# Swapping which engine multiplies two tiles by C in a scan kernel, and retiming the streams beside it

## The chip, the core and the metric

The kernel runs on one core of a Trainium2 chip. The metric is the device time of one execution in microseconds; the time of a kernel is the median of its runs. In the text PE is the matrix engine, DVE the vector engine, ACT the scalar engine, POOL GpSimd, and SP the engine whose queue issues the DMAs. Each engine takes its own instructions strictly in the order in which the program wrote them, and waits on semaphores where an operand isn't ready.

## What is computed

The reference takes eight images of 96 channels and 64 x 64 pixels through two layers. The first is a layer norm, a projection, a depthwise convolution with silu, then a selective scan in four directions over 4096 positions, a gate with silu(z), an output projection, a skip, and a convolutional channel attention with gelu. The second is attention without softmax and a feed forward with float8 rounding. Nearly all of the time goes into the scan:

```
def step(hst, inp):
    u_i, dt_i, b_i, c_i = inp
    dA = jnp.exp(dt_i[..., None] * A)
    hst = dA * hst + (dt_i * u_i)[..., None] * b_i[:, :, None, :]
    y = jnp.einsum('bkdn,bkn->bkd', hst, c_i)
    return (hst, y)
```

There are 192 channels d, 16 states n, four directions k and eight images.

## The kernel before

**Units, tiles, slots.** A chunk is 512 positions. A unit is one chunk in one direction of one image: 8 images x 4 directions x 8 chunks = 256 units, 32 per image. A unit has six tiles. A tile `hb` is 128 rows (64 channels, two states) by 4 x 512 (four states m): 128x2048. `TILES` orders them g = 0, 1 (groups of states), and in each j = 0, 1, 2 (groups of channels), so tile n and tile n + 3 have the same channels. A unit is emitted in 24 slots, one for each row m of each tile.

For a tile the steps are:

- `inputs` (L998, POOL): hb = B x du, the product with B. In the texts this is I0 to I5 by tile.
- `decays` (L1123, ACT): da = exp(delta x A) into one of four PSUM banks, issued two slots ahead of its scan.
- the scan (L1195, DVE), one per slot, 512 positions with a carry from the unit before.
- the product with C. `BANKED` says for each tile how many of its four rows DVE multiplies: there the scan writes to the bank `da`, DVE multiplies the bank by C one slot later (L1201), and ACT copies the carry (L1202). The rest is done by POOL at once for all rows left, in place (`outputs`, L1004; O0 to O5 by tile), after ACT has copied the carry (L1207).
- `sums` (L1024, PE): sums over the states. `gather` (L1046, L1049, ACT) takes the sums from PSUM.

`BANKED` has two rows; the first is for the first eight units of an image (but not of image 0), the second for all others. Before, DVE has tiles 0, 2 and 4 whole and two or three rows of tile 5; POOL has tiles 1 and 3 and the rest of tile 5.

**The plan.** `plan` writes out by hand, for each of the 24 slots, what is emitted after that slot's scan: sums and gather of the unit before, `inputs` of coming tiles, `states` (DMAs of B and C, L932), `step_sizes` (L963 on PE, L971, L973 and L975 on ACT, L977 on DVE, L980 on POOL: softplus of dt, and dt x u) for a unit two ahead, and `spread` (DMAs of delta and du, L992). Since engines are in order, the plan sets each engine's queue. Before, POOL's queue in a unit is O5 of the unit before, I2, I3, O1, I4, the product for `ua`, I5, in odd units the product for `ub`, O3, then I0 and I1 of the next unit.

**The streams.** The other stages of the network are Python generators that run beside the scan. `advance` ticks a clock after each slot and lets each stream emit its next step; a step yields the number of ticks to its successor (`PA` = 2 after a matmul). `later` puts a DMA `HOLD` = 3 ticks off, and `fetch` marks its target as landed `LAND` = 11 ticks after the request; `landed` yields ticks until then. In images 1 to 7 the back stream works on the image before, on `kit_b`, one chunk after another: `gated` (L446 to L476), `first_conv`, `second_conv`, the channel gate, `attention`, `joined`, `feed_forward`. The front stream prepares the next image (`normed`, `paired`) at 1.5 ticks for one. `norm` (L253 to L259, then L246 and L247) is a helper of many stages. `quiet` holds a silu or gelu, which needs two table loads on ACT (L275), until the slot is in `CALM`.

In `gated` a chunk is centred by PE (L446, L447), squared by ACT (L449) and multiplied by z on DVE (L450), first 128 rows, then 64; then comes a variance, the projection (L462, L463), its scaling on DVE (L465), and a norm. Streams have one PSUM bank each (`f0`, `f1`); the dt matmul of `ua` shares the bank `y01` with the sums of tiles 0, 1, 3 and 4, and that of `ub` shares `y2` with those of tiles 2 and 5.

After the last unit come the last gated chunk and the other back stages of image 7, on four kits side by side.

Of the kernel before, what the change touches and what calls it, by code (L numbers as in the profile page):

```python
# [12 lines left out]
AF = mybir.ActivationFunctionType  # L13
# [6 lines left out]
B, C, HW = 8, 96, 64  # L20
# [10 lines left out]
SPREAD = 5  # L31
HB = 6

BANKED = ((4, 0, 4, 0, 4, 2), (4, 0, 4, 0, 4, 3))

HOLD = 3
LAND = 11
# [1 line left out]
PA = 2  # L39
# [4 lines left out]
def kernel(ctx: ExitStack, tc: tile.TileContext, a, out):  # L44
# [8 lines left out]
    nc = tc.nc  # L53
# [105 lines left out]
    def landed(*parts):  # L159
        while clock[0] < max(p.ready for p in parts):  # L160
            yield 1
# [56 lines left out]
    def windowed(ap):  # L218

        return ap.rearrange("p (w i j) -> p i w j", w=8, i=8)  # L220

    def raster(ap):
        return ap.rearrange("p (i w j) -> p i w j", i=8, w=8)

    def square(ap):
        return ap.rearrange("p (r w) -> p r w", r=8)
# [22 lines left out]
    def norm(k, srcs, sq, d):  # L249

        ps = bank(k.tag, "ctr")[:C, :]
        for i, src in enumerate(srcs):
            nc.tensor.matmul(ps, cen_c, src, start=i == 0, stop=i == len(srcs) - 1)  # L253
        yield PA
        nc.scalar.activation(sq, ps, AF.Square)
        nc.scalar.copy(d, ps)  # L256
        yield 1
        ps = bank(k.tag, "var")[:C, :]
        nc.tensor.matmul(ps, ones_c, sq, start=True, stop=True)  # L259
        yield PA  # L260
        inv_std(ps, ps)
        yield 1
        return ps

    alone = [False]
    place = [None]
    CALM = (0, 1, 8, 9, 16, 17)

    def quiet():

# [135 lines left out]
    def back_end(b, s):  # L406
# [8 lines left out]
        def gated(k, cs):  # L415


            def fetch_y(c):
                fetch(k.ya, s["y"][0][0:P, bass.ts(c, T)])
                fetch(k.yb, s["y"][0][P:DY, bass.ts(c, T)])  # L420

            def fetch_z(c):
                fetch(k.za, s["zd"][0:P, bass.ts(c, T)])
                fetch(k.zb, s["zd"][P:DI, bass.ts(c, T)])

            def fetch_base(c):
                fetch(k.bs, s["base"][:, bass.ts(c, T)])

            bs, r = k.bs.t[:C], k.r[:C]
            full, low, up, early = slice(0, P), slice(0, 64), slice(64, P), 0  # L430
            for n, c in enumerate(cs):
                while c not in s["done"]:
                    yield 1
                if n == 0 or early < n:
                    fetch_y(c)
                if n == 0:
                    fetch_z(c)
                    fetch_base(c)
                after = cs[n + 1] if n + 1 < len(cs) else None
                yield from landed(k.ya, k.yb, k.za, k.zb, k.bs)  # L440
                for rows, (wa, wb_), z, sq in (
                    (full, (cen_aa, cen_x), k.za.t, k.s1),
                    (up, (cen_x[:, 0:64], cen_bb), k.zb.t, k.s2[up]),
                ):
                    ps = bank(k.tag, "dy")[rows, :]
                    nc.tensor.matmul(ps, wa, k.ya.t, start=True, stop=False)  # L446
                    nc.tensor.matmul(ps, wb_, k.yb.t, start=False, stop=True)  # L447
                    yield PA
                    nc.scalar.activation(raster(sq), windowed(ps), AF.Square)  # L449
                    nc.vector.tensor_tensor(raster(z), windowed(ps), raster(z), ALU.mult)  # L450
                    yield 1
                if after in s["done"]:
                    fetch_y(after)
                    early = n + 1
                ps = bank(k.tag, "var")[:C, :]
                nc.tensor.matmul(ps, cen_x[:, 0:C], k.s1, start=True, stop=False)
                nc.tensor.matmul(ps, cen_x[up, 0:C], k.s2[up], start=False, stop=True)
                yield PA
                inv_std(r, ps, -1.0)
                yield 1  # L460
                ps = bank(k.tag, "attn")[:C, :]
                nc.tensor.matmul(ps, wy[0], k.za.t, start=True, stop=False)  # L462
                nc.tensor.matmul(ps, wy[1][up], k.zb.t, start=False, stop=True)  # L463
                yield PA
                nc.vector.tensor_tensor(r, ps, r, ALU.mult)  # L465
                if after is not None:
                    fetch_z(after)
                later(x1d[:, bass.ts(c, T)], r)
                if early == n and after in s["done"]:
                    fetch_y(after)  # L470
                    early = n + 1
                yield 1
                rs = yield from norm(k, (r, bs), k.s1[:C], k.d1[:C])
                if after is not None:
                    fetch_base(after)
                nc.vector.tensor_tensor(k.pad[0:C, :, 1 : HW + 1], square(k.d1[:C]), square(rs), ALU.mult)  # L476
                if early == n and after in s["done"]:
                    fetch_y(after)
                    early = n + 1
                later(xld[:C, 1 + 8 * c : 9 + 8 * c, :], k.pad)  # L480
                if k.solo and n == 5:
                    fetch_rows(k.im, xld, NC - 2)
                yield 1
# [42 lines left out]
        def second_conv(k, cs):  # L526
            if not k.solo:
                for p, c in zip(k.m3, cs):
                    nearer(p, c)
            for n, c in enumerate(cs):  # L530
                yield from landed(k.m3[n % 2])
                ps = bank(k.tag, "cab2")[:C, :]
                for dx in range(3):
                    nc.tensor.matmul(  # L534
                        ps, cab2_w[:, dx, :], k.m3[n % 2].t[:, :, dx : dx + HW], start=dx == 0, stop=dx == 2
                    )
                    if dx == 1:
                        yield 1
                yield PA
                if n + 2 < len(cs):  # L540
                    nearer(k.m3[n % 2], cs[n + 2])
                t = (k.s1, k.d1)[n % 2][:C]
                nc.scalar.activation(t, ps, AF.Identity, bias=cab2_b)
                yield 1
                nc.vector.tensor_reduce(totals[:, c : c + 1], t, AX.X, ALU.add)
                later(td[:, bass.ts(c, T)], t)
                if n == len(cs) - 1:
                    sources(k, cs[0])
                yield 1
# [29 lines left out]
        def attention(k, cs):  # L579

            t, x1, bs, new = k.ya.t[:C], k.za.t[:C], k.bs.t[:C], k.r[:C]
            for n, c in enumerate(cs):
# [27 lines left out]
                for i in range(4):  # L610
                    part = lnt[:, i * (C + 1) : (i + 1) * (C + 1)]
                    nc.tensor.matmul(ps, part, part, start=i == 0, stop=i == 3)  # L612
                yield PA
                nc.vector.tensor_tensor(gram, ps, gram, ALU.add)
                if n == len(cs) - 1:
                    normed_again(k, 0, cs[0])
# [23 lines left out]
        def feed_forward(k, cs):  # L640

            for n, c in enumerate(cs):
# [1 line left out]
                yield from landed(k.ln, k.t2[n % 2])  # L644
                ps = bank(k.tag, "att")[:C, :]
                nc.tensor.matmul(ps, small["qkvf"], k.ln.t, start=True, stop=True)  # L646
                yield PA
                nc.vector.scalar_tensor_tensor(t, ps, bff, t, ALU.add, ALU.add)
                if n + 1 < len(cs):
                    normed_again(k, n + 1, cs[n + 1])  # L650
# [406 lines left out]
    def plan(u, last, nxt, third, fourth):  # L1057
# [3 lines left out]
        def put(slot, f, *args):  # L1061
            at[slot].append((f, args))

        if last:
            put(0, outputs, last, 5)
            for m in range(2):
                put(m, sums, last, (3, 4), 2 + m)
            for m in range(2):
                put(3 + m, sums, last, (5,), m)
            put(3, gather, last, 0)  # L1070
            put(7, states, u, 1, 1)
            put(7, gather, last, 1)
        for n in range(6):
            to = (u, n + 2) if n < 4 else (nxt, n - 4)
            if to[0]:
                put(4 * n + 1, inputs, *to)
        if third and u.i % 2:
            put(16, step_sizes, (nxt, third), 5)
        put(8, outputs, u, 1)
        put(16, outputs, u, 3)  # L1080
        for m in range(4):
            put(13 + m, sums, u, (0, 1), m)
            if m < 2:
                put(18 + m, sums, u, (2,), m)
                put(22 + m, sums, u, (3, 4), m)
        put(18, before, u)
        if nxt:
            put(0, spread, nxt, 0, (0, 1))
# [7 lines left out]
        if third:  # L1096
            if third.i < NC:
                put(0, fetched_dt, third)
            put(5, fetched_u, third)
            for i, slot in enumerate((6, 8, 9, 10, 11, 12)):  # L1100
                put(slot, step_sizes, (third,), i)
            if u.i % 2:
                for i, slot in enumerate((9, 11, 12, 13, 15)):
                    put(slot, step_sizes, (nxt, third), i)
                put(17, spread, nxt, 0, (2,))
                put(18, spread, nxt, 1, (2,))
            elif u.i + 3 < len(units):
                put(21, fetched_pair, third, units[u.i + 3])
# [194 lines left out]
```

## Time and profile before

| what | value |
|---|---|
| median of 3 runs | 10766.89 us (10758.35 to 10770.26) |
| the profiled execution's own time | 10764.72 us |
| its span | 10763.0 us |
| granted TensorE clock, mean | 0.841 |
| ACT busy | 7397.8 us (69%) |
| DMA queue q1, share of 16 engines | 84.5% |
| scan L1195, mean of one | 1205 to 1274 ns by form |

The span is cut into 40 slices on the page; DVE and POOL show 9 (90% or more) in all but the first and the last:

```profile
DVE  3999999999999999999999999999999999999993
ACT  4666666777676776777767776677766767666674
POOL 3999999999999999999999999999999999999991
```

A group's line reads: line, engine, operation, out<-in, shapes and count, then busy time in us and mean ns of one, then the time the engine stood idle just before these instructions and what ended it. A line of waits reads: who waited, for whom, total us, times, longest. A line of windows gives the stretch, its length, busy time and count for PE, PEld (weight loads), DVE, ACT and POOL, then the granted clock, the DMA share and GB/s. Busy times of a group can overlap a little at both ends, so that three scans of 1.27 in a row take 3.6 us.

### The profile page before, as it was taken

Reading aid. Unit: us, or ns where it says so; the run is one execution under the profiler, and the core shown is the slowest. Engines: PE = TensorE matmul, PEld = TensorE weight load, DVE = VectorE, ACT = ScalarE, POOL = GpSimd, SP = SyncE. Lnnn points to the kernel's source line nnn. Section 1 sums busy time; section 2 is a strip of 40 time slices with the busy share of each in tenths; the row PEclk is TensorE's granted clock in tenths of the full one; section 3 lists DMA queues with packets and bytes.
Section 4 is the critical chain, followed back from the end, with each engine's and each line's share of the span. In section 5 each row is a group of like instructions: output and inputs, shape, how many; then the busy total and the mean of one; then the engine's idle time right before and its main releaser. Section 6 shows DMA issues by size and latency. Waiting matters only on the chain. (4 is left out here: it accounts for less than half of the span.)

```text
span 10763.0 us, 97608 instructions
## 1 busy us (share of the span) xinstructions
PE 8423.7 (78%) x23270; PEld 2274.2 (21%) x23270; DVE 10158.1 (94%) x11126; ACT 7397.8 (69%) x15154; POOL 10118.0 (94%) x2782
## 2 busy tenths in 40 slices
PE   7777668886788867888688886888768887677677
PEld 2121112221122211222122221222112221111112
DVE  3999999999999999999999999999999999999993
ACT  4666666777676776777767776677766767666674
POOL 3999999999999999999999999999999999999991
PEclk8888788987889878998789887898778987778788
DMA  6888888998889988898888988889888898888883
GB/s 148 208 205 209 200 209 214 226 226 200 215 216 227 227 193 220 216 231 219 201 218 214 237 212 202 217 220 237 198 211 218 219 235 200 202 203 210 208 214 94
DMA packets 1095381, 2253.29 MB, mean 209 GB/s; under 512 B 435993, under 2 KB 436698, under 8 KB 963731
## 3 DMA queue, kind: packets, MB, share of 16 engines
q1 hardware_dynamic: 1094803, 2247.05, 84.5%
q8 instruction: 184, 3.01, 0.1%
q14 instruction: 394, 3.23, 0.1%
HBM read 1507.14 MB, written 336.69 MB: 171 GB/s over the span
## 5 line engine op out<-in xcount | busy, mean ns | idle before, releaser
L998 POOL TENSOR_TENSOR hb<-b,du 128x2048 f32<-128x2048 f32 x1536 | 6952.6, 4546 | 6.1 <-DMA du<-ua 5.2
L1024 PE MATMUL p<-hb,halves 128*64 128x512 f32 x12288 | 3713.8, 707 | 1053.0 <-POOL hb L1004 562.6
L1123 ACT ACTIVATE da<-delta,w_a_logs 128x512 f32<-128x512 f32 x6144 | 4164.3, 689 | 541.5 <-DVE hb L1195 447.5
L1195 DVE TENSOR_TENSOR_SCAN da<-da,carry,hb 128x512 f32<-128x512 f32 x3311 | 4164.0, 1274 | 90.7 <-ACT carry L1202 37.0
L1004 POOL TENSOR_TENSOR hb<-hb,c 128x2048 f32<-128x2048 f32 (+2 forms) x768 | 2714.3, 3534 | 222.3 <-ACT carry L1207 203.0
L1195 DVE TENSOR_TENSOR_SCAN hb<-da,carry,hb 128x512 f32<-128x512 f32 x2065 | 2547.0, 1265 | 1.8
L1201 DVE TENSOR_TENSOR hb<-da,c 128x512 f32<-128x512 f32 x3784 | 2534.0, 670 | 1.8 <-DMA c<-xd 0.9
L1202 ACT COPY carry<-da 128x1 f32<-128x1 f32 x3784 | 593.8, 157 | 2054.5 <-DVE hb L1201 2045.1
L1024 PEld LDWEIGHTS p<-hb,halves 128*64 128x64 f32 x12288 | 904.8, 157 | 3697.8 <-issue 1876.0
L313 PE MATMUL conv<-f0im,taps 97*128 97x512 f32 (+1 forms) x2088 | 867.7, 655 | 37.2 <-ACT f0pre L369 32.2
L1195 DVE TENSOR_TENSOR_SCAN da<-da,hb 128x512 f32<-128x512 f32 x473 | 566.1, 1214 | 28.0 <-POOL hb L998 26.6
L963 PE MATMUL dt<-dts,dt_w 7*128 7x512 f32 (+1 forms) x1024 | 485.9, 742 | 92.3 <-ACT carry L1207 36.2
L980 POOL TENSOR_TENSOR ua<-nat,ua 128x512 f32<-128x512 f32 x256 | 329.9, 1289 | 170.9 <-DVE nat L977 161.8
L313 PEld LDWEIGHTS conv<-f0im,taps 97*128 97x128 f32 (+1 forms) x2088 | 256.4, 173 | 588.2 <-issue 508.8
L1207 ACT COPY carry<-hb 128x4 f32<-128x4 f32 (+2 forms) x768 | 149.7, 195 | 302.1 <-DVE hb L1195 293.7
L1195 DVE TENSOR_TENSOR_SCAN hb<-da,hb 128x512 f32<-128x512 f32 x295 | 346.8, 1205 | 1.7 <-ACT carry L1202 1.7
L259 PE MATMUL var<-f1e,ones_c 96*96 96x512 f32 x350 | 225.6, 731 | 121.8 <-ACT f1e L256 68.5
L253 PE MATMUL ctr<-f1e,cen_c 96*96 96x512 f32 x402 | 218.1, 649 | 86.1 <-ACT f1e L592 34.2
L977 DVE SCALAR_TENSOR_TENSOR nat<-dt,nat 128x512 f32<-128x512 f32 x384 | 258.0, 672 | 17.9 <-ACT nat L975 12.7
L975 ACT ACTIVATE nat<-nat,one 128x512 f32<-128x512 f32 x384 | 271.8, 708 | 0.1
L497 PE MATMUL cab<-f1im,cab_w 97*32 97x512 f32 x1044 | 256.0, 603 | 12.5 <-DMA f1im<-xld 7.1
L275 ACT ACT_TABLE_LOAD x193 | 247.6, 1283 | 4.1 <-PEq L1292 0.8
(430 smaller groups left out, 7586.0 us busy)
## 6 DMA issues: line engine op xcount, KB each, us to landing
b<-xd SPq DMA_DIRECT2D x1024, 512.0 KB
c<-xd SPq DMA_DIRECT2D x1024, 512.0 KB
delta<-nat SPq DMA_DIRECT2D x1536, 128.0 KB
du<-ua SPq DMA_DIRECT2D x1024, 128.0 KB
y<-yt SPq DMA_DIRECT2D x512, 256.0 KB
u<-y SPq DMA_DIRECT2D x384, 256.0 KB
ua<-u SPq DMA_DIRECT2D x256, 256.0 KB
du<-ub SPq DMA_DIRECT2D x512, 128.0 KB
```

Of the source, the lines that this page charges most:

```text
L313: nc.tensor.matmul(ps, taps[:, t, lo : lo + n], im[:, r0 + dy : r0 + dy + 8, dx : dx + HW], start=t == 0, stop=t == 8,)
L963: nc.tensor.matmul(ps, dt_w.rearrange("r j d -> r (j d)")[32 * w.k : 32 * w.k + R + 1, d], w.dts, start=True, stop=True)
L975: nc.scalar.activation(u.nat, u.nat, AF.Ln, bias=one)
L977: nc.vector.scalar_tensor_tensor(u.nat, u.ps, 0.0, u.nat, ALU.max, ALU.add)
L980: nc.gpsimd.tensor_tensor(x, u.nat, x, ALU.mult)
L998: nc.gpsimd.tensor_tensor(hb, u.bc[0, g], u.du[j].unsqueeze(1).to_broadcast([P, G, T]), ALU.mult)
L1004: nc.gpsimd.tensor_tensor(hb, hb, u.bc[1, TILES[n][0]][:, lo:, :], ALU.mult)
L1024: nc.tensor.matmul(ps, halves, u.hb[n][:, i, :], start=TILES[n][0] == 0 and m == 0, stop=False, skip_group_check=True)
L1123: nc.scalar.activation(da[q], u.delta[j], AF.Exp, scale=a_neg[:, u.k, j, g * G + m : g * G + m + 1])
L1195: nc.vector.tensor_tensor_scan(dd if banked else x, dd, x, 0.0 if u.start else col, ALU.mult, ALU.add)
L1201: nc.vector.tensor_tensor(x, d, c, ALU.mult)
L1202: kept.append(lambda: nc.scalar.copy(col, d[:, at : at + 1]))
```

## The change

The change has two halves.

In the scan, `BANKED` gives tile 0's products with C to POOL and tile 1's to DVE. POOL's queue becomes: O5 of the unit before, I2, O0, I3, I4, I5, the product for `ua`, I0 of the next unit, in odd units the product for `ub`, O3, I1 of the next unit. The sums of tiles 0 and 1 are emitted two slots earlier, those of tile 2 one slot; gather 0 one slot later and gather 1 one slot earlier; the step sizes one or two slots earlier.

In the streams, the slots for silu and gelu change, `norm`, `second_conv`, `attention` and `feed_forward` get one tick more ahead of a DVE step, and in `gated` the multiply by z is emitted a tick ahead of the square, z and base are awaited where they are first used, and the next base is fetched earlier.

```diff
--- before.py
+++ after.py
@@ -31,7 +31,7 @@
 SPREAD = 5
 HB = 6
 
-BANKED = ((4, 0, 4, 0, 4, 2), (4, 0, 4, 0, 4, 3))
+BANKED = ((0, 4, 4, 0, 4, 2), (0, 4, 4, 0, 4, 3))
 
 HOLD = 3
 LAND = 11
@@ -259,12 +259,12 @@
         nc.tensor.matmul(ps, ones_c, sq, start=True, stop=True)
         yield PA
         inv_std(ps, ps)
-        yield 1
+        yield 2
         return ps
 
     alone = [False]
     place = [None]
-    CALM = (0, 1, 8, 9, 16, 17)
+    CALM = (4, 5, 16, 17, 18, 19)
 
     def quiet():
 
@@ -437,7 +437,7 @@
                     fetch_z(c)
                     fetch_base(c)
                 after = cs[n + 1] if n + 1 < len(cs) else None
-                yield from landed(k.ya, k.yb, k.za, k.zb, k.bs)
+                yield from landed(k.ya, k.yb)
                 for rows, (wa, wb_), z, sq in (
                     (full, (cen_aa, cen_x), k.za.t, k.s1),
                     (up, (cen_x[:, 0:64], cen_bb), k.zb.t, k.s2[up]),
@@ -446,9 +446,11 @@
                     nc.tensor.matmul(ps, wa, k.ya.t, start=True, stop=False)
                     nc.tensor.matmul(ps, wb_, k.yb.t, start=False, stop=True)
                     yield PA
-                    nc.scalar.activation(raster(sq), windowed(ps), AF.Square)
+                    yield from landed(k.za, k.zb)
                     nc.vector.tensor_tensor(raster(z), windowed(ps), raster(z), ALU.mult)
                     yield 1
+                    nc.scalar.activation(raster(sq), windowed(ps), AF.Square)
+                yield 1
                 if after in s["done"]:
                     fetch_y(after)
                     early = n + 1
@@ -461,7 +463,7 @@
                 ps = bank(k.tag, "attn")[:C, :]
                 nc.tensor.matmul(ps, wy[0], k.za.t, start=True, stop=False)
                 nc.tensor.matmul(ps, wy[1][up], k.zb.t, start=False, stop=True)
-                yield PA
+                yield PA + 1
                 nc.vector.tensor_tensor(r, ps, r, ALU.mult)
                 if after is not None:
                     fetch_z(after)
@@ -470,9 +472,12 @@
                     fetch_y(after)
                     early = n + 1
                 yield 1
-                rs = yield from norm(k, (r, bs), k.s1[:C], k.d1[:C])
+                yield from landed(k.bs)
+                steps = norm(k, (r, bs), k.s1[:C], k.d1[:C])
+                yield next(steps)
                 if after is not None:
                     fetch_base(after)
+                rs = yield from steps
                 nc.vector.tensor_tensor(k.pad[0:C, :, 1 : HW + 1], square(k.d1[:C]), square(rs), ALU.mult)
                 if early == n and after in s["done"]:
                     fetch_y(after)
@@ -541,7 +546,7 @@
                     nearer(k.m3[n % 2], cs[n + 2])
                 t = (k.s1, k.d1)[n % 2][:C]
                 nc.scalar.activation(t, ps, AF.Identity, bias=cab2_b)
-                yield 1
+                yield 2
                 nc.vector.tensor_reduce(totals[:, c : c + 1], t, AX.X, ALU.add)
                 later(td[:, bass.ts(c, T)], t)
                 if n == len(cs) - 1:
@@ -610,7 +615,7 @@
                 for i in range(4):
                     part = lnt[:, i * (C + 1) : (i + 1) * (C + 1)]
                     nc.tensor.matmul(ps, part, part, start=i == 0, stop=i == 3)
-                yield PA
+                yield PA + 1
                 nc.vector.tensor_tensor(gram, ps, gram, ALU.add)
                 if n == len(cs) - 1:
                     normed_again(k, 0, cs[0])
@@ -644,7 +649,7 @@
                 yield from landed(k.ln, k.t2[n % 2])
                 ps = bank(k.tag, "att")[:C, :]
                 nc.tensor.matmul(ps, small["qkvf"], k.ln.t, start=True, stop=True)
-                yield PA
+                yield PA + 1
                 nc.vector.scalar_tensor_tensor(t, ps, bff, t, ALU.add, ALU.add)
                 if n + 1 < len(cs):
                     normed_again(k, n + 1, cs[n + 1])
@@ -1063,26 +1068,27 @@
 
         if last:
             put(0, outputs, last, 5)
-            for m in range(2):
-                put(m, sums, last, (3, 4), 2 + m)
+            for m in range(2, 4):
+                put(m - 2, sums, last, (3, 4), m)
             for m in range(2):
                 put(3 + m, sums, last, (5,), m)
-            put(3, gather, last, 0)
+            put(4, gather, last, 0)
+            put(6, gather, last, 1)
             put(7, states, u, 1, 1)
-            put(7, gather, last, 1)
-        for n in range(6):
+        put(4, outputs, u, 0)
+        for n, slot in enumerate((0, 5, 8, 11, 15, 19)):
             to = (u, n + 2) if n < 4 else (nxt, n - 4)
             if to[0]:
-                put(4 * n + 1, inputs, *to)
+                put(slot, inputs, *to)
         if third and u.i % 2:
             put(16, step_sizes, (nxt, third), 5)
-        put(8, outputs, u, 1)
         put(16, outputs, u, 3)
         for m in range(4):
-            put(13 + m, sums, u, (0, 1), m)
-            if m < 2:
-                put(18 + m, sums, u, (2,), m)
-                put(22 + m, sums, u, (3, 4), m)
+            put(11 + m, sums, u, (0, 1), m)
+        for m in range(2):
+            put(17 + m, sums, u, (2,), m)
+        for m in range(2):
+            put(22 + m, sums, u, (3, 4), m)
         put(18, before, u)
         if nxt:
             put(0, spread, nxt, 0, (0, 1))
@@ -1097,10 +1103,10 @@
             if third.i < NC:
                 put(0, fetched_dt, third)
             put(5, fetched_u, third)
-            for i, slot in enumerate((6, 8, 9, 10, 11, 12)):
+            for i, slot in enumerate((5, 7, 8, 9, 10, 12)):
                 put(slot, step_sizes, (third,), i)
             if u.i % 2:
-                for i, slot in enumerate((9, 11, 12, 13, 15)):
+                for i, slot in enumerate((8, 10, 11, 12, 13)):
                     put(slot, step_sizes, (nxt, third), i)
                 put(17, spread, nxt, 0, (2,))
                 put(18, spread, nxt, 1, (2,))
```

## The prediction

> **What bounds the kernel now.** I read the page's shares first, then the groups, then windows over one image, then the waits inside these windows.
>
> ```profile
> span 10763.0 us, 97608 instructions
> PE 8423.7 (78%) x23270; PEld 2274.2 (21%) x23270; DVE 10158.1 (94%) x11126; ACT 7397.8 (69%) x15154; POOL 10118.0 (94%) x2782
> ```
>
> DVE and POOL are level, so no one engine is the bound. The scan stage (first L1195 at 181.0 us, last one's end at 10532.6) is 10351.6 us of the span; the rest is the start and a tail of 230 us. The groups say what the two do.
>
> ```profile
> L998 POOL TENSOR_TENSOR hb<-b,du 128x2048 f32<-128x2048 f32 x1536 | 6952.6, 4546 | 6.1 <-DMA du<-ua 5.2
> L1004 POOL TENSOR_TENSOR hb<-hb,c 128x2048 f32<-128x2048 f32 (+2 forms) x768 | 2714.3, 3534 | 222.3 <-ACT carry L1207 203.0
> L1201 DVE TENSOR_TENSOR hb<-da,c 128x512 f32<-128x512 f32 x3784 | 2534.0, 670 | 1.8 <-DMA c<-xd 0.9
> ```
>
> Over 256 units that is 6 products with B and 3 with C per unit on POOL, and 24 scans with 14.8 products on DVE. POOL waited 203 us for the carry copy L1207, that is for DVE to end a tile. Now image 3 (units 96 to 127, 4042.6 to 5341.7 us) cut at its unit 0, the gated chunks, the middle, and the feed forward; columns are PE, PEld, DVE, ACT, POOL.
>
> ```profile
> 4042.60:4080.80 38.20, 21.74 (x55) 6.22 (x52) 36.58 (x40) 22.29 (x49) 38.20 (x11) 0.76 0.96 233
> 4080.80:4458.00 377.20, 315.66 (x807) 81.68 (x806) 358.94 (x391) 258.39 (x533) 359.17 (x96) 0.86 0.87 217
> 4458.00:5018.00 560.00, 490.30 (x1494) 135.57 (x1492) 549.93 (x602) 404.77 (x818) 544.61 (x149) 0.92 0.90 225
> 5018.00:5341.70 323.70, 214.37 (x556) 55.19 (x558) 319.12 (x346) 240.06 (x500) 323.11 (x94) 0.75 0.82 200
> sum 1299.10, PE 1042.07 PEld 278.66 DVE 1264.56 ACT 925.50 POOL 1265.09; mean PE 260.52 PEld 69.67 DVE 316.14 ACT 231.38 POOL 316.27
> ```
>
> In the first and last row POOL idles 0.0 and 0.6 us: POOL-bound. In the two middle rows DVE needs 908.9 and POOL 903.8 of 937.2 us, and both idle some 30 us. Who starts it? DVE's waits there, then POOL's:
>
> ```profile
> DVE f1x L450 <- ACT f1e L449: 8.8, 5, 4.2
> DVE da L1195 <- ACT carry L1202: 6.1, 3, 3.2
> DVE f1pre L450 <- ACT f1pre L449: 4.8, 7, 0.9
> DVE f1e L465 <- PE attn L463: 3.4, 3, 2.1
> DVE f1ln L597 <- ACT var L247: 2.0, 2, 1.3
> DVE da L1195 <- POOL hb L998: 1.4, 1, 1.4
> ```
> ```profile
> POOL hb L1004 <- ACT carry L1207: 26.4, 21, 2.4
> ```
>
> DVE waits for POOL only 1.4 us. It loses its time to the side streams (L450, L465, L597) and to ACT busy with table loads (L1195 behind L1202), and POOL's 26.4 us follow from that. So units 1 to 23 are DVE plus its stalls, units 24 to 0 are POOL. A gain must come from DVE's stalls, or from POOL entering unit 24 further ahead.
>
> **The change part by part, per image.**
>
> *The product with C moved from tile 1 to tile 0.* Three products on POOL and 14 or 15 on DVE remain, in the same shapes: 0 us of work. What moves is POOL's order:
>
> ```profile
> 5026.31 1.30 POOL L1004 TENSOR_TENSOR hb<-hb,c 128x512 f32<-128x512 f32 x1
> 5027.53 9.04 POOL L998 TENSOR_TENSOR hb<-b,du 128x2048 f32<-128x2048 f32 x2
> 5037.17 4.52 POOL L1004 TENSOR_TENSOR hb<-hb,c 128x2048 f32<-128x2048 f32 x1 [0.59 <-ACT carry L1207]
> ```
>
> O5 of the unit before (1.3), I2, I3 (4.5 each), then O1, 10.3 us after O5 began. (O is a product with C, I one with B, the digit the tile.) In DVE's timeline a slot with a product takes 1.78 us and one without 1.19, so tiles 0 and 1 end 4 x 1.78 + 4 x 1.19 = 11.9 us into the unit, more with side work: POOL waits unless O5 began 1.6 to 2.3 us late. After: O5, I2, O0, 5.8 us after O5 began, while tile 0, now without products, ends at 4 x 1.19 = 4.8. O5 itself then is what holds POOL, and POOL may run 2 us further ahead. With O5 at t (about 1), the other deadlines hold: I3 ends t+14.8 for tile 3 at 19.0; I4 t+19.3 for 23.8; I0 of the next unit, now ahead of O3, t+29.5 for 39; I1 t+39.1 for 43.7. Before, the tightest were I0 (t+34.6 for 38.9) and I4, but with t held at 2. The room for jitter grows from about 2 to 3.2 us. I count the lead once per image, where units 24 on start to eat it: **-2**.
>
> O3 now ends at t+34.6; the sums of slot 22, at about 36.7, read it. While t is under 2 nothing waits; later PE does, with the side streams' matmuls queued behind. That is in POOL-bound units, where DVE waits anyway. The product for `ub` goes from t+25 to t+30, so SP, which already waits for it (183.1 us in 96 waits), stands 4 us longer in odd units; behind it are the `du` copies (needed at t+41, about 10 us later) and B of the second group (needed 15 us later): 0.
>
> *dt in slots 5 to 13, gather in 4 and 6.* The dt matmul follows gather 0 by one slot instead of three. PE's waits of L963 for L1049 (33.6 us in 28, in the view of waits) can grow; DVE reads dt only in slot 10. Between 0 and 0.6 us (a copy, L1049 0.578) in each unit on PE, none on DVE: 0.
>
> *The gated chunk.* Square L449 and the multiply L450 read one bank, and the trace lets L450 start only when L449 ends. With L450 first it waits for PE alone. L450 lost 13.6 us here; 4.8 of it (L450 on 64 rows, 0.7 each) is just the Square's length. In the 8.8, ACT itself waited for PE (57 us in 29 waits over the run, 1.9 each), which stays. But z and base are now awaited where they are used: counting yields, a chunk takes 22 ticks instead of 29 (the trace shows L450 moving 5 slots per chunk: 29 = 24 + 5), so gated ends in slot 6 of unit 8 instead of slot 4 of unit 10. It so misses the two units that hold 3.3 and 4.2 of the stalls, where the silu of the front stream falls. Against it: the second dy matmul is issued in the same tick as the Square that frees its bank, so PE has two slots (2.4 to 3.6 us) for a Square (0.59) and four passes (2.1). Bounds 2 to 12 left; I take 6, close to half as the PE part is: **-7.6**. L465 gets three slots instead of two: 3.4 to 1.4, **-2.0**.
>
> *One tick more in norm, second conv, gram and att.* L597 2.0, L653 0.8, L476 0.6: 3.4 to 1.0, **-2.4**. Back stages last 5 ticks more per chunk or less, against 46 won before; they ended in slot 6 of unit 31, so no drain is added.
>
> *Tables in slots 4, 5, 16 to 19.* A silu is 1.28 + 1.48 + 1.28 = 4.0 us on ACT. `decays` runs two slots ahead, so with three slots with products DVE has 5.3 us, and ACT needs 4.0 + 0.16 + 0.69 = 4.9: just covered. Slots 4 to 11 and 16 to 22 all have products now. The 6.1 us came where other ACT work or a gelu met it, which can still happen: 6.1 to 3.5 (bounds 0 and 9), **-2.6**.
>
> The row for a table load is 1283 ns (L275, 193 loads). The Trainium skill, ScalarE: Activation LUTs, section "Table sets: the hidden batching unit", puts a switch between sets at about 2.7 us per load. By that a silu would be 2 x 2.7 + 1.5 = 6.9 us, over the cover of 5.3 by 1.6, some 19 us per image for 12 pairs, and the change would lose; the trace has half that figure (as has a measured one in that page's section "What ACT_TABLE_LOAD costs"), and I go by the trace.
>
> *What it adds.* Slots 23 and 0 to 3 (22 too in the first eight units) are now five or six in a row without product: 7.1 us for DVE, while ACT needs 6 x 0.63 = 3.8 for its exps plus side work, on average (925.5/32 - 24 x 0.63)/40.4 = 0.34 of the time, 2.4 us: 6.2, covered on average. Bunched, I take **+2** (0 to 23). Gated packed into fewer units leaves units 9 to 12 POOL-bound by about 0.7 us each: **+3** (0 to 6). The tail's extra ticks issue no instruction: 0, by the 230 us there at most 5 either way.
>
> Sum: -2 - 7.6 - 2.0 - 2.4 - 2.6 + 2 + 3 = -11.6 us per image. Images 1 to 7: -81; image 0 has no gated, -2. The profiled execution took 10764.7, so 10682; the median of the runs is 2.2 above it: **10684 us**.
>
> **Rivals.**
> *A, all of it:* L450 falls to 2, L465, norm and tables to 0, nothing new; -2 - 11.6 - 3.4 - 3.4 - 6.1 + 3 = -23.5 per image, 10600. For it: the room for jitter. Against: ACT's waits for PE are real.
> *B, PE takes the Square's place:* L450 gives 3, L465 and tables nothing, norm 1.4, lead 2, with +2 and +3: -1.4 per image, 10757. For it: PE was busy 490 of 560 us in the middle, and gated now comes denser.
> *C, half works* (bank turn-around costs what L450 saves): -6 per image, 10724.
> *D, slower:* ACT starves DVE in slots 22 to 3. It decides from the point where side work in that run exceeds 3.3 us plus the two exps of lead (2.4), 5.7 us; a norm (2.3) beside two evictions (1.2) and a transposed gather (1.1) stays below by 1.1. At 1 us in each of units 1 to 23, +161, less 83: 10845.
> That the change misses its aim (POOL's waits vanish, the time doesn't move, as POOL isn't the bound in units 1 to 23) is part of B.
>
> **Chances.** Forecast 0.47, A 0.17, C 0.07, B 0.17, D 0.12. A measurement of this kernel tells about 0.2% (21.5 us) from no change. Faster: 0.47 + 0.17 + 0.07 = 0.71; same 0.17; slower 0.12. The range goes from A to a little past B: 10600 to 10780.
>
> **What would show it.** L1004's wait for L1207 falls from 203 us to under 80; L450's sum from 90 to under 45, released by PE; L597 and L653 nearly gone; L1195's wait for L1202 at 15 to 30; L998 and L1201 keep their counts and means; POOL idles least in units 24 to 0 as now. Wrong if DVE's L1195 waits for L1123 in slots 0 to 3 by tens of us, if L450 waits for PE as long as for L449 before, or if POOL's share doesn't rise.

## The result and the profile after

The changed kernel takes 10895.3 us (median of 4 runs, 10894.0 to 10897.4) against 10763.9 us for the kernel before, run beside it (4 runs, 10758.4 to 10770.3): ratio 1.0122, 95% interval 1.0105 to 1.0140. It is slower by 1.2%, where the forecast was 0.7% faster; the time lies 115 us above the range.

The page of the changed kernel, shares of the engines:

```profile
span 10894.3 us, 98150 instructions
PE 8223.4 (75%) x23270; PEld 2245.3 (21%) x23270; DVE 10211.3 (94%) x11126; ACT 7416.2 (68%) x15154; POOL 10117.4 (93%) x2782
```

POOL's work is as it was (10118.0 before). DVE has 53 us more of busy time with the same 11126 instructions, so some of them last longer. Now windows of image 3 of the changed kernel, cut at the same units as before (0, 1 to 8, 8 to 24, 24 to 31; columns PE, PEld, DVE, ACT, POOL):

```profile
4092.20:4130.10 37.90, 21.51 (x58) 5.39 (x58) 36.57 (x41) 22.86 (x51) 37.90 (x11) 0.77 0.99 226
4130.10:4474.00 343.90, 294.25 (x794) 76.52 (x796) 329.89 (x361) 235.43 (x492) 326.22 (x87) 0.90 0.88 220
4474.00:5082.00 608.00, 491.23 (x1462) 137.81 (x1458) 585.02 (x633) 431.59 (x866) 576.23 (x157) 0.88 0.89 219
5082.00:5409.40 327.40, 211.95 (x597) 55.67 (x596) 320.73 (x347) 237.53 (x490) 325.02 (x94) 0.77 0.81 196
sum 1317.20, PE 1018.94 PEld 275.39 DVE 1272.21 ACT 927.40 POOL 1265.37; mean PE 254.74 PEld 68.85 DVE 318.05 ACT 231.85 POOL 316.34
```

Image 3 takes 1317.2 us instead of 1299.1. DVE is busy 1272.2 instead of 1264.6, 7.6 more, and idle 45.0 instead of 34.5, 10.5 more. So the loss has two parts of like size: an instruction that got longer, and waits. The waits of DVE in units 1 to 23:

```profile
DVE da L1201 <- ACT da L1129: 27.1, 14, 6.0
DVE f1x L450 <- PE dy L447: 4.8, 1, 4.8
DVE f1pre L450 <- PE dy L447: 2.6, 1, 2.6
```

Against the list of before, L465, L597 and L653 are gone and L450 is down from 13.6 to 7.4 us, as forecast. But the scans now wait 27.1 us for their exps on ACT, where before they waited 6.1 behind L1202.

The longer instruction is one per image: `dgate`, the identity matrix times a gate for each channel, 96x96, in the channel gate. Its row in the kernel before, then in the changed one:

```profile
L572 DVE TENSOR_SCALAR dgate<-ident,gate x8: 266/3771/3777, 2123.4 to 10648.6; 96x96 f32<-96x96 f32 x8
```
```profile
L577 DVE TENSOR_SCALAR dgate<-ident,gate x8: 265/11738/11752, 2065.7 to 10774.8; 96x96 f32<-96x96 f32 x8
```

The columns are shortest, median and longest. The shortest is image 7's, in the tail, where POOL has no scan work: 0.27 us. In the seven other images it lasts 3.8 us before and 11.7 after. Here it is in image 3 of the changed kernel, with the 96x1 instruction of the same kind that runs just ahead of it, and then what POOL does meanwhile:

```profile
4700.46 0.15 DVE L575 TENSOR_SCALAR gate<-gate 96x1 f32<-96x1 f32 x1
4700.83 11.74 DVE L577 TENSOR_SCALAR dgate<-ident,gate 96x96 f32<-96x96 f32 x1
```
```profile
4699.10 4.50 POOL L1003 TENSOR_TENSOR hb<-b,du 128x2048 f32<-128x2048 f32 x1
4703.56 4.49 POOL L1009 TENSOR_TENSOR hb<-hb,c 128x2048 f32<-128x2048 f32 x1
4708.02 4.49 POOL L1003 TENSOR_TENSOR hb<-b,du 128x2048 f32<-128x2048 f32 x1
4725.40 1.27 POOL L1009 TENSOR_TENSOR hb<-hb,c 128x512 f32<-128x512 f32 x1 [12.90 <-ACT carry L1213]
```

Three products follow each other without a gap and end at 4712.51; `dgate` ends at 4712.57. Here DVE stood until POOL ran out of work, and POOL ran out because its next product needs a scan of the very DVE that stands.

### The profile page after: what moved, and what is told of

It is laid out like the page before. It is cut to its first block, busy times and chain, and to the rows that moved or that the text cites. A ratio compares the mean times of both kernels' runs of the same rounds, so it can differ in the third digit from the quotient of the medians.

```text
span 10894.3 us, 98150 instructions
## 1 busy us (share of the span) xinstructions
PE 8223.4 (75%) x23270; PEld 2245.3 (21%) x23270; DVE 10211.3 (94%) x11126; ACT 7416.2 (68%) x15154; POOL 10117.4 (93%) x2782
## 5 line engine op out<-in xcount | busy, mean ns | idle before, releaser
L1003 POOL TENSOR_TENSOR hb<-b,du 128x2048 f32<-128x2048 f32 x1536 | 6943.2, 4537 | 143.4 <-issue 99.9
L1009 POOL TENSOR_TENSOR hb<-hb,c 128x2048 f32<-128x2048 f32 (+2 forms) x768 | 2706.6, 3524 | 248.4 <-ACT carry L1213 192.7
L968 PE MATMUL dt<-dts,dt_w 7*128 7x512 f32 (+1 forms) x1024 | 426.1, 630 | 37.1 <-ACT carry L1208 12.9
L1054 ACT COPY yt<-p 128x512 f32<-128x512 f32 x368 | 213.5, 580 | 131.7 <-PE p L1034 68.5
L982 DVE SCALAR_TENSOR_TENSOR nat<-dt,nat 128x512 f32<-128x512 f32 x384 | 257.2, 670 | 24.9 <-ACT nat L980 13.3
```

The source lines that it names most:

```text
L968: nc.tensor.matmul(ps, dt_w.rearrange("r j d -> r (j d)")[32 * w.k : 32 * w.k + R + 1, d], w.dts, start=True, stop=True)
L1003: nc.gpsimd.tensor_tensor(hb, u.bc[0, g], u.du[j].unsqueeze(1).to_broadcast([P, G, T]), ALU.mult)
L1009: nc.gpsimd.tensor_tensor(hb, hb, u.bc[1, TILES[n][0]][:, lo:, :], ALU.mult)
```

## What made the exps late

Unit 18 of image 3 has the longest such wait (6.0 us). Follow it backwards through the changed kernel. ACT:

```profile
4843.52 1.92 ACT L1129 ACTIVATE da<-delta,w_a_logs 128x512 f32<-128x512 f32 x3
4854.01 0.58 ACT L597 COPY f1e<-x 96x512 f32<-96x512 f32 x1 [8.57 <-PE x L591]
```

ACT has issued the exps up to two slots ahead, and then a copy out of PSUM for the back stream, L597, holds its queue for 8.57 us, waiting for PE. PE:

```profile
4840.36 1.97 PE L1029 MATMUL p<-hb,halves 128*64 128x512 f32 x4 [3.80 <-POOL hb L1009]
4842.26 2.08 PE L313 MATMUL conv<-f0im,taps 97*128 97x512 f32 x2
4844.27 1.98 PE L1029 MATMUL p<-hb,halves 128*64 128x512 f32 x4
4846.17 2.02 PE L591 MATMUL x<-f1x,dgate 96*96 96x512 f32 x2
```

The sums of tiles 3 and 4 stood at the head of PE's queue and waited 3.80 us for O3 (L1009). Behind them stood convs and L591. And what came after ran slowly: windows just after the wait and then on, where the third number from the end is the granted clock:

```profile
4840.30:4851.50 11.20, 11.14 (x16) 2.73 (x16) 8.93 (x10) 3.15 (x8) 10.17 (x4) 0.50 0.95 241
4851.50:4857.00 5.50, 5.50 (x16) 1.79 (x16) 1.79 (x2) 2.81 (x6) 1.63 (x1) 0.93 0.38 114
```

After its wait PE had half its clock: 16 matmuls in 11.2 us, then 16 in 5.5. Cut finer, the granted clock is 1.00 until 4838.58, 2.0 us after PE's last matmul had ended, then 0.50 until 4852.23, 11.9 us after PE had resumed, and 1.00 again after that. The Trainium skill, TensorE: Matmul & The Clock Gate, "Part 1: The HAM clock gate", gives an idle window of about 3.4 us for the halving and at least one busy window of that length for the release. Here the halving came sooner, and more than three such windows of unbroken work passed before the release; the measurement decides. The slow clock lengthens such a stretch, but the change didn't add to it over the run: its mean is 0.841 before and 0.840 after.

Last, POOL at that time:

```profile
4830.09 4.53 POOL L1003 TENSOR_TENSOR hb<-b,du 128x2048 f32<-128x2048 f32 x1 [1.25 <-DMA base<-f0e]
4834.58 1.27 POOL L985 TENSOR_TENSOR ub<-nat,ub 128x512 f32<-128x512 f32 x1
4835.80 4.50 POOL L1009 TENSOR_TENSOR hb<-hb,c 128x2048 f32<-128x2048 f32 x1
```

The first line is I0 of the next unit. It stands ahead of O3 now, and it waited itself, 1.25 us. Over the run POOL idled 143.4 us ahead of products with B, nearly all of it ahead of an I0; before it was 6.1:

```profile
L1003 POOL TENSOR_TENSOR hb<-b,du 128x2048 f32<-128x2048 f32 x1536 | 6943.2, 4537 | 143.4 <-issue 99.9
```

"Issue" says that the profile names no engine, and the name in brackets above is not the cause either. I0 takes the buffer of this unit's tile 0, which comes free when PE has summed it, and in 8 of the 9 units of image 3 where I0 waited over 0.15 us it starts 0.13 to 0.14 us after the last matmul of those sums. So there is a ring: PE late with the sums, I0 late, O3 behind it late, PE late with the next sums, at half clock. PE's waits of the sums for POOL's product with C over the run, before and after:

```profile
PE p L1024 <- POOL hb L1004: 562.6, 189, 9.3
```
```profile
PE p L1029 <- POOL hb L1009: 1017.1, 196, 14.9
```

## Theory and rival

Theory 1: the plan costs it. O3 behind I0 makes PE wait, PE makes ACT wait, and ACT's late exps make DVE wait; beside it `dgate` stands while POOL works. Theory 2: the stream half costs it, with its denser gated chunks. My own rival D (slots 22 to 3 without products starve DVE) is refuted by the trace already: of 30.6 us per image that scans waited for ACT in images 1 to 6 (idle time ahead of each scan, by slot), slots 5 to 9 have 20, slot 19 has 7.4, and slots 22 to 3 under 1.

## Experiments

Medians are of 4 runs or more. The kernel before was run again beside each group of experiments (1 to 4, 5 to 8, 9 to 12) and took 10764.9, 10766.9 and 10764.7 us. Ratios are to it, with 95% intervals.

**1. The scan half alone.** `BANKED`, `plan` and `CALM` as changed, the streams as before.

> The scan half alone: BANKED, plan and CALM of the changed kernel, streams of before. Theory 1 (the loss comes from the plan: O3 behind I0 makes PE wait, and silus sit behind gather 0 and the carry copy of tile 0): most of the loss is here, 10820 to 10890 us, and PE's wait of the sums for O3 is 90 us or more per image, against 58 before. Theory 2 (the stream half is at fault: its denser gated chunks): at or under the kernel before, 10730 to 10770.

Measured 10912.7 us, ratio 1.0132 (1.0115 to 1.0149), a little over the upper end. PE's sums waited 105 us for POOL's product with C per image (58 before). `dgate` took 0.27 us in most images here, and the time was still the longest of all: the waits alone can lose as much. Theory 2 falls.

**2. The stream half alone.** The yields and `gated` as changed, the rest as before.

> The stream half alone: yields, gated's new order and waits of the changed kernel; BANKED, plan and CALM of before. Theory 1: the gains that I forecast for the streams appear, -8 to -12 us per image, 10680 to 10710; L450's waits fall to 30 to 50 us over the run. Theory 2: 10850 or more. The dgate instruction can land anywhere between 0.3 and 12 us, by what POOL does just then, so +-55 us stay open until its length is read.

Measured 10757.3 us, 0.9993 (0.9983 to 1.0002): no change, which neither theory gave. But DVE's waits fell from 34.6 to 27.1 us per image and L450's from 98.7 to 20.3 us over the run, while `dgate` rose from 3.8 to 11.4 us. The gain is there, and `dgate` would account for what took it back, which 7 tests. The rows of `dgate` in 1 and in 2:

```profile
L572 DVE TENSOR_SCALAR dgate<-ident,gate x8: 266/267/6726, 2154.4 to 10800.8; 96x96 f32<-96x96 f32 x8
```
```profile
L577 DVE TENSOR_SCALAR dgate<-ident,gate x8: 265/11428/11453, 2051.3 to 10640.8; 96x96 f32<-96x96 f32 x8
```

So the changed streams make it long even under the old plan, and the scan half alone doesn't. In the kernel before and in 1 it comes in slot 14 of unit 16 of an image, in 2 in slot 0 of unit 15 and in the changed kernel in slot 16 of unit 14, where POOL has several products to do one behind the other.

**3. `dgate` on ACT** in the changed kernel.

```diff
-            nc.vector.tensor_scalar(dgate, ident[:C, :C], gate, None, ALU.mult)
+            nc.scalar.activation(dgate, ident[:C, :C], AF.Identity, scale=gate)
```

> The changed kernel with one instruction per image moved: dgate (ident times gate, 96x96) on ACT instead of DVE. In the changed kernel this DVE instruction lasts 11.7 us in each of images 0 to 6 (3.8 before) and ends when POOL first has a gap. If DVE is held by POOL, and that time is lost: 7 x 11.4 = 80 us less at most, 10815 to 10840. If the time is made up later, since POOL's own wait after it (10.8 us per image) only moves: 10880 to 10895.

Measured 10820.0 us, 1.0052 (1.0037 to 1.0067): 75 us less, nearly all of the 80 that it held DVE. On ACT it takes 0.375 us.

**4. I0 behind O3** in the changed kernel.

```diff
-        for n, slot in enumerate((0, 5, 8, 11, 15, 19)):
+        for n, slot in enumerate((0, 5, 8, 11, 17, 19)):
```

> The changed kernel with the next unit's first product with B emitted in slot 17, behind O3, instead of 15, ahead of it. Theory 1: PE's wait of the sums for O3 falls from 103 us per image to 70 or less, the waits of L450 for PE in unit 1 (7.7 us per image) and of ACT for PE in unit 18 (8.6) go, -8 to -15 us per image: 10790 to 10840. If the order of O3 and I0 is not what costs: 10880 to 10910.

Measured 10713.5 us, 0.9954 (0.9940 to 0.9969): 182 us less by one number, far beyond my expectation, and faster than before. PE's wait of the sums fell from 103 to 43 us per image. `dgate` fell from 11.7 to 3.5 us too: 57 of the 182 are that. Here it ended with the one product of POOL that ran when it began, in all seven images, though the next product followed without a gap. In image 3:

```profile
4637.42 3.47 DVE L577 TENSOR_SCALAR dgate<-ident,gate 96x96 f32<-96x96 f32 x1
```
```profile
4636.31 4.51 POOL L1009 TENSOR_TENSOR hb<-hb,c 128x2048 f32<-128x2048 f32 x1 [0.64 <-ACT carry L1213]
4640.79 9.00 POOL L1003 TENSOR_TENSOR hb<-b,du 128x2048 f32<-128x2048 f32 x2
```

So DVE doesn't always need a gap on POOL, and after which product it gets its turn stays open.

**5. Both remedies.**

> Both remedies in the changed kernel: I0 of the next unit in slot 17, behind O3, and dgate on ACT. With O3 ahead alone the time was 10713 us and dgate still held DVE for 3.5 us in each image. If the two losses are separate: 10713 - 7 x 3.1 = 10691 (10680 to 10700). If dgate's time is taken back by other waits: 10705 to 10715.

Measured 10694.2 us, 0.9931 (0.9916 to 0.9946): they add up. With `dgate` on ACT on both sides, the place of I0 is worth 10820.0 - 10694.2 = 126 us, 18 per image. DVE's waits between these two runs fall by about as much (per image, from images 1 to 6): the scans' for ACT from 30.3 to 19.5 us, L450's from 10.0 to 2.3, L653's from 2.6 to 0. The line that answers for it, PE's waits in units 1 to 23 of image 3, in the changed kernel and then here:

```profile
PE p L1029 <- POOL hb L1009: 51.1, 15, 11.6
```
```profile
PE p L1029 <- POOL hb L1009: 6.9, 3, 4.9
```

**6. Another `CALM`**, added to 5.

```diff
-    CALM = (4, 5, 16, 17, 18, 19)
+    CALM = (5, 6, 17, 18, 19)
```

> The same with CALM = (5, 6, 17, 18, 19): silu and gelu no longer in slots 4 and 16, where ACT's queue first holds the carry copy of a tile without products (it waits for that tile's last scan) and, in 4, gather 0. If it is that place that costs, DVE's waits for the exps in slots 7 and 19 fall (13 us per image with O3 ahead), by 4 to 8 us per image: 10635 to 10665. If a silu costs the same in any slot, the waits move one slot on: 10680 to 10700. The streams shift by some ticks against the slots, which can move other waits by some us.

Measured 10697.7 us, 0.9937 (0.9922 to 0.9951): nothing gained. The waits moved by a slot and shrank a little: 4.9 us per image in slot 7 became 4.4 in slot 8, and 9.1 in slot 19 became 7.0 in slot 20. All of the scans' waits for ACT fell from 19.5 to 14.3 us, but the other waits of DVE rose by 7, half of that at L450 (2.3 to 5.7), as the streams shifted against the slots. So this place of the silu is not what holds the time up; what it costs by itself isn't separated here from the shift.

**7. The stream half with `dgate` on ACT.**

> The stream half alone (10757 us, the same as before) with dgate on ACT. There dgate held DVE for 11.4 us per image, and DVE's other waits fell from 34.6 to 27.1 us per image. If the stream half is good for 7 us per image and dgate took it back: 10757 - 7 x 11 = 10680 (10670 to 10700). If not: 10735 or more.

Measured 10677.5 us, 0.9915 (0.9899 to 0.9932), as expected. It is 17 us under 5, which has the swap of the tiles, the new plan and the new `CALM` beside the same streams.

**8. The scan half with both remedies**, the streams as before.

> The scan half alone, with I0 behind O3 and dgate on ACT; streams of before. It says what the swap of the two tiles is worth when O3 isn't held up. By my forecast POOL's room for jitter and the lead were worth 2 us per image, and DVE is the bound in units 1 to 23, with the streams' stalls of before: 10735 to 10765, with dgate's 3.8 us per image of before (27 us) gone in it. If the swap is worth more by itself: under 10720. If slots without products in a row starve DVE: over 10780.

Measured 10740.2 us, 0.9975 (0.9965 to 0.9984), in the expected range. 9, which leaves out the whole scan half, is 4.6 us slower, and their intervals overlap: beside the old streams the swap is worth nothing that can be shown. Beside the new streams the scan half costs time even with O3 ahead: 17 us between 7 and 5, and 24 between 11 and 12.

**9. The kernel before with `dgate` on ACT.**

> The kernel before with dgate on ACT. It held DVE for 3.8 us in each of seven images there. If all of that is lost time: 10766 - 7 x 3.4 = 10742 (10735 to 10750). If POOL is the bound around unit 16 and the time is taken back: 10760 or more.

Measured 10744.8 us, 0.9981 (0.9972 to 0.9991): the 3.8 us per image were lost time before as well.

**10. `dgate` on DVE from PSUM**, in the changed kernel.

```diff
+            eye = bank(k.tag, "eye")[:C, :C]
+            nc.tensor.matmul(eye, ident[:C, :C], ident[:C, :C], start=True, stop=True)
             yield 1
...
-            nc.vector.tensor_scalar(dgate, ident[:C, :C], gate, None, ALU.mult)
+            nc.vector.tensor_scalar(dgate, eye, gate, None, ALU.mult)
```

> The changed kernel with dgate still on DVE, in the same place, but its source is a copy of ident in PSUM that one more matmul per image makes there. If what holds dgate is that DVE's form with its one source and its result in SBUF can't start while POOL's products follow each other without a gap: it falls from 11.7 to 0.2 to 0.4 us, and the time to that with dgate on ACT, 10810 to 10830. If any DVE instruction of that place is held: it stays at several us and the time at 10870 to 10900.

Measured 10800.8 us, 1.0038 (1.0023 to 1.0053), 9 us under the expected range and 19 under 3; what the further 19 are is not shown. The row of the instruction in this kernel:

```profile
L579 DVE TENSOR_SCALAR dgate<-eye,gate x8: 314/314/314, 2076.2 to 10693.3; 96x96 f32<-96x96 f32 x8
```

Same engine, same operation, same place, beside a POOL as busy, and 0.314 us in all eight images. So it is not DVE's place in the plan but the source, in SBUF or in PSUM. Nor is a source and a result in SBUF enough by itself: L575, 96x1, has both there and took 0.15 us just ahead of `dgate`. The Trainium skill, SBUF — State Buffer, "Who interferes with whom", says that `tensor_scalar` in its two-port mode and GpSimd exclude each other for the length of an instruction. VectorE: DVE Perf Modes, "Why PSUM operands drop a tier", says that an operand in PSUM rules this mode out. That agrees with 0.3 against 11.7 us, though no run shows in which mode `dgate` ran. The traces show more: in the kernel before, in 2 and in the changed kernel DVE didn't get its turn until POOL stood, over parts of four products in 2; in 4 it got it behind the first.

**11 and 12. Silu and gelu kept apart**, added to 7 and to 5.

```diff
+    free_at = [0]
...
-        while place[0] is not None and place[0] not in CALM:
+        while place[0] is not None and (place[0] not in CALM or clock[0] < free_at[0]):
             yield 1
+        free_at[0] = clock[0] + 6
```

What called for it is this stretch of ACT in unit 11 of image 3 of the changed kernel:

```profile
4576.82 1.28 ACT L275 ACT_TABLE_LOAD   x1
4578.12 0.68 ACT L515 ACTIVATE gm<-cab,cab_b 64x512 f32<-64x512 f32 x1
4578.82 2.57 ACT L275 ACT_TABLE_LOAD   x2
4581.40 1.48 ACT L321 ACTIVATE f0pre<-f0pre 128x1536 f32<-128x1536 f32 x1
4582.90 1.28 ACT L275 ACT_TABLE_LOAD   x1
4584.20 0.69 ACT L1129 ACTIVATE da<-delta,w_a_logs 128x512 f32<-128x512 f32 x1
```

`quiet` lets both streams go in the first slot that is in `CALM`, so a gelu and a silu keep the next exp waiting for 7.4 us, against 5.3 us of cover. A table load takes 1.3 us here from the instruction ahead of it to the one behind it, as the prediction had it.

> The stream half alone with dgate on ACT (10678 us), and after a silu or gelu has passed, the next one waits for a CALM slot at least 6 ticks later, so that a silu and a gelu don't stand on ACT one behind the other. DVE's waits for ACT (19 us per image) hold the pairs in units 11 and 16, some 6 us. If the meeting of the two is what costs: 4 to 6 us per image less, 10630 to 10655. If each costs by itself: 10670 to 10690.

Measured 10646.0 us, 0.9891 (0.9875 to 0.9908), 32 us less than 7, as expected. It is the fastest of all, 1.1% under the kernel before, and has the old plan.

> The changed kernel with I0 behind O3, dgate on ACT (10694 us), and silu and gelu kept 6 ticks apart as well. The pair in unit 11 waits 4.3 us in slot 19; without it 4 to 6 us per image less: 10650 to 10670. If a silu and a gelu apart cost as much as together: 10685 to 10700.

Measured 10670.1 us, 0.9912 (0.9897 to 0.9927), 24 us less than 5, at the upper end of what was expected.

## Why the prediction was wrong, point by point

Per image, from images 1 to 6 (their period rose from 1300.1 to 1317.6 us), forecast and measured:

| term | forecast | measured |
|---|---|---|
| L450 | -7.6 | 13.3 to 7.7: -5.6 |
| L465 | -2.0 | 2.7 to 0: -2.7 |
| L597, L653, L476 | -2.4 | 3.6 to 2.3 (L653, for PE): -1.3 |
| scans waiting for ACT | -2.6, and +2 for slots 22 to 3 | 7.9 to 30.6: +22.7 |
| scans waiting for POOL (the lead) | -2 | 6.0 to 1.2: -4.8 |
| gated packed, POOL-bound units | +3 | not seen |
| `dgate` | not in the sum | 3.8 to 11.7: +8.0 |

The measured terms add up to +16.3 of the +17.5 us by which the period rose. The terms of the streams were right in sign, -12.0 forecast and -9.6 measured. Freed of the rest they are larger: between 9 and 7 the waits at L450, L465 and L597 fall by some 19 us per image, while the scans wait 12 us longer for ACT (7.2 to 19.3), so that the streams are worth 67 us net (10744.8 to 10677.5), 9.6 per image. The lead shows as shorter waits for POOL but not as time: 8 against 9 gains nothing that can be shown. Rival D, slower at 10845, had the right side by luck; the cause that it gave is the one the trace refutes. Of the three signs of being wrong only POOL's share showed itself (94 to 93%), and L1009's wait for its carry copy was 192.7 us, not under 80. Three steps failed.

The first is "O3 now ends at t+34.6; the sums of slot 22, at about 36.7, read it. While t is under 2 nothing waits; later PE does ... That is in POOL-bound units, where DVE waits anyway." The margin of 2 us was too thin to put at 0. On average t was 1.9 us (O5 started that long after its unit), and I0, which I had taken as free to run, waited for PE's sums; O3 began 33.0 us into its unit on average, not at t+30.1 = 32.0. PE waited 103 us per image, in units 1 to 23 too, and the streams behind PE held ACT's queue, in which the exps stand. By experiment the place of I0 costs 18 us per image. I had weighed only who reads O3, not who in turn sets I0 free.

The second is what I left out. The wait view shows no wait for `dgate`, so I took the row L572 (8 of them, 3332 ns mean) for its cost and passed it over. A 96x96 operation of 3.8 us beside 512-wide products of 0.67 should have been asked what it stood for. What I booked as a gain is what made it longer: the faster streams bring `dgate` forward, to a stretch where POOL's products follow each other (11.4 us in 2, which has the stream half alone, against 0.27 in most images of 1, which has the scan half alone). By experiment its whole stand costs 75 us in the changed kernel (3) and 20 in the kernel before (9).

The third is the term for the tables, "6.1 to 3.5 (bounds 0 and 9), -2.6". Of the +22.7 us that the scans wait longer for ACT, 10.7 are undone by I0's place (5 against 3) and 12 stay. The new streams bring most of these by themselves: in 2, with the old plan and the old `CALM`, the scans wait 17.8 us for ACT, against 7.9 before. The cover of 5.3 us against 4.9 is not enough for a silu with a gelu (7.4); 6 shows that one slot later is no better, 11 and 12 that keeping the two apart is worth 32 and 24 us, about 4 per image. What makes up the rest of the 12 is open.

What stays open besides: how the 18 us share out between O3 coming one product later and I0's own wait. A seventh `hb` buffer, which would take the wait alone away, wasn't tried.

## What to carry to other kernels

When a product is moved ahead in an in-order queue, follow both ends of what falls behind it: who waits for that, and what sets the moved one's own buffer free; if the two meet on one engine, a margin like the 2 us here is none. Where two engines are both busy nearly all the time, look for instructions that last far longer than their size: they may be standing while the other engine works, and the view of waits doesn't show it. Before a stage's forecast gain is booked, look for a single instruction that can take it back.

## What the runs showed of the hardware

- A 96x96 `tensor_scalar` on DVE with source and result in SBUF stood 11.7 us, over three POOL products in a row, and ended when POOL idled; in 4 it took 3.5 us and ended with the first product, though the next followed at once. From PSUM it took 0.314 us, on ACT 0.375 us, and a 96x1 one from SBUF to SBUF 0.15 us.
- PE's clock was granted at 0.50 from 2.0 us into a wait of 3.8 us until 11.9 us after it, with PE busy 11.14 of 11.20 us; the 512-column sums took 1.06 us in it instead of 0.59.
- The products kept their mean lengths to 1% from the kernel before to the changed one (with B on POOL 4546 and 4537 ns, with C on DVE 670 and 668 ns): the new order made `dgate` longer and these products not. Whether the two engines slow each other alike in both kernels, no run here shows.
